# An attention layer's last pair of heads: output projection inside the slots, all blocks turned on VectorE, divisions in smaller groups

## The chip, the cores and the metric

The kernel runs on one core of one Trainium2 chip. The metric is the device time of one execution in microseconds (us); lower is better. All arithmetic is in 32-bit floating point.

## The reference

Two layers over 4096 nodes with 512 features each. Layer 0 is an additive graph attention, layer 1 is a masked dot-product attention with 8 heads of 64. Both add their result to their input.

```python
# layer 1, on h = relu(layernorm(x)), x of 4096 x 512, adj of 4096 x 4096
keys    = einsum('nj,hjk->hnk', h, Wks)        # 8 heads of 64
queries = einsum('nj,hjk->hnk', h, Wqs)
values  = einsum('nj,hjk->hnk', h, Wvs)
atts = einsum('hqk,hmk->hqm', queries, keys) / 8
atts = atts - 1e16 * (1 - maximum(adj, eye))
atts = softmax(atts, axis=-1)
out = x + einsum('hqm,hmk,hko->qo', atts, values, Wo)
```

The change lies in layer 1 only: in its last part, where heads 6 and 7 are worked on, and in the product with Wo that ends the kernel.

## The kernel before

**Stages.** Layer 0 runs first, in three pairs of heads and then a fourth pair whose stage also makes keys, queries and values of layer 1. Then comes layer 1, the subject here, from about 2490 us to the end. Its work goes over HC = 4 *pairs* of heads. Each pair has NG = 32 *groups* of 128 queries, each group has GS = 4 *slots* of 32 queries, so a pair has SETS = 128 slots and the layer `total` = 512. One loop over s (L1205 and above) hands out the work of a slot, written out by hand: instructions are issued to each engine in the order of the program. In this text, slots are counted within the last pair: slot 0 of it is s = 384, and the tail begins at slot 128.

**One slot's work.** The 128 partitions hold 4 quarters of the 4096 keys times 32 queries; the free axis holds QK_ = 1024 keys, for two heads.
- `scores` (L997): TensorE makes the products of queries and keys into four PSUM tiles `sc` of 128x512, one slot's worth; the pool has four buffers.
- `masked` (L1013): VectorE adds the penalty tile `a` (loaded by SP from pen_d, 512 KB a slot, five slots ahead, pool "a" with six buffers), writes to the ring `t` in SBUF and keeps the minima.
- `parted` (L1022) on GpSimd, `smallest` (L1034 on TensorE, L1039 on VectorE): every second slot, the minimum over the four quarters.
- `exps` (L1050): ScalarE takes the exponential, in place, three slots behind, and keeps the sums in `sums`.
- `squares` (L1057): four slots behind, VectorE turns squares of 32x32 in the first VC = 768 columns of both heads (128x1536 elements).
- `turned` (L1065) and `taken` (L1072): the other 256 columns are turned on TensorE in 128x128 blocks, for two slots at a time into a PSUM tile `tr` of two banks, and copied back by ScalarE.
- `weighted` (L1083): eight slots behind, TensorE multiplies with the values, 32 products a slot, into the PSUM tile `o` of a group. Values for the columns turned on TensorE are loaded in another order of rows.
- `finish` (L1092): ScalarE copies `o` out, SP writes it to att_d in DRAM.

**Divisions.** The softmax is divided by its sums late. `due` puts a generator into a list when enough groups are made; `some_divided` carries it on by one step in each slot. `inverted` sums over quarters, inverts, turns and writes to inv_d. `scaled` loads att_d and the inverses, multiplies (GpSimd, L1134; for the last groups VectorE) and writes att_d back. In the last pair there are divisions of 16, 8 and 8 groups.

**The tail.** After the last slot, `projected` multiplies, for each of NB = 32 blocks of 128 rows, the four pairs' columns of att_d with Wo (`wot`): four products of 128x512 into one `sc` tile (L1188), VectorE adds them to the rows of x (L1191), and SP stores. `load_chunk` loads two blocks of att_d and of x at a time. In the first eight tail slots the weighted products of the last groups stand between the blocks.

Of the kernel before, what the change touches and what calls it, by code (L numbers as in the profile page):

```python
# [15 lines left out]
P = 128  # L16
# [7 lines left out]
def kernel(  # L24
# [76 lines left out]
    with tc.tile_pool(name="a0k", bufs=1) as pk, tc.tile_pool(name="a0v", bufs=4) as pv, tc.tile_pool(  # L101
# [68 lines left out]
        def exps(G, h):  # L170
            if h == 0:
                G.sm = psb.tile([P, 2], F32, name="sm")
            nc.scalar.activation(  # L173
                G.t[h], G.t[h], AF.Exp, bias=G.nm[h][:, NCH : NCH + 1], scale=-1.0,
                accum_out=G.sm[:, h : h + 1],
            )
# [286 lines left out]
        def step(n):  # L463
            return groups[n // 2], n % 2
# [126 lines left out]
    with tc.tile_pool(name="b0c", bufs=1) as pc, tc.tile_pool(name="b0a", bufs=4) as pa, tc.tile_pool(  # L591
# [42 lines left out]
        def load_values(i):  # L634
            v = pv.tile([P, MB, PR], F32, name="bv")
            for a in range(NS):
                rows = bass.ds(a * QK_ + i * MB * SQ, MB * SQ)
                nc.sync.dma_start(
                    v[bass.ts(a, SQ)], d1_d[rows, bass.ts(C3, PR)].rearrange("(n i) d -> i n d", i=SQ)
                )  # L640
            values.append(v)
# [257 lines left out]

    HF = QK_ // 2
    VC = 768
    NV = VC // SQ
    NT = (QK_ - VC) // P
    SG = NG // 2
    with tc.tile_pool(name="a1t", bufs=1) as pt, tc.tile_pool(name="a1k", bufs=4) as pkk, tc.tile_pool(
        name="a1v", bufs=GS
    ) as pv, tc.tile_pool(name="a1a", bufs=6) as pa, tc.tile_pool(name="a1q", bufs=2) as pq, tc.tile_pool(
        name="a1x", bufs=2  # L910
    ) as px, tc.tile_pool(name="a1s", bufs=6) as psb, tc.tile_pool(name="a1z", bufs=2) as pz, tc.tile_pool(name="a1at", bufs=3) as pat, tc.tile_pool(
        name="a1sc", bufs=4, space=PSUM
    ) as psc, tc.tile_pool(name="a1tr", bufs=1, space=PSUM) as ptr, tc.tile_pool(
        name="a1m", bufs=1, space=PSUM
# [4 lines left out]
        class Group:  # L919


            def __init__(self, c, g):
                self.c, self.g = c, g
                self.ring = (c * NG + g) % (RING // GS) * GS
                self.nm = {}
                self.parts = {}

# [9 lines left out]
                )  # L937
                keys[c].append(k)

        def load_values(c, i):  # L940

            v = pv.tile([P, MB, PR], F32, name="v")
            cols = bass.ts(c, PR)
            if i * MB < NV:
                for a in range(NS):
                    rows = bass.ds(a * QK_ + i * MB * SQ, MB * SQ)
                    nc.sync.dma_start(
                        v[bass.ts(a, SQ)], v_d[rows, cols].rearrange("(n i) d -> i n d", i=SQ)
                    )
            else:  # L950
                for m in range(NT):
                    nc.sync.dma_start(
                        v[:, bass.ts(m, NS), :],
                        v_d[:, cols].rearrange("(a m p) d -> m p a d", a=NS, p=P)[VC // P + m],
                    )
            values[c].append(v)
# [96 lines left out]
                )  # L1053

        def squares(G, k):
            u = t[:, G.ring + k, :, :VC].rearrange("p h (n j) -> p h n j", j=SQ)
            nc.vector.transpose(u, u)  # L1057

        def turned(G, k):
# [14 lines left out]
        def weighted(G, i):  # L1074
            if i == 0:
                G.o = po.tile([P, 512], F32, name="o")
            v = values[G.c][i]
            for b in range(MB):
                mb = i * MB + b

                at = mb * SQ
                for h in range(2):
                    nc.tensor.matmul(  # L1083
                        G.o[bass.ts(h, D), :P],
                        lhsT=v[:, b, bass.ts(h, D)],
                        rhs=t[:, bass.ds(G.ring, GS), h, bass.ds(at, SQ)],
                        start=(mb == 0), stop=(mb == NB - 1),
                    )

        def finish(G):  # L1090
            oT = px.tile([P, P], F32, name="oT")
            nc.scalar.copy(oT, G.o[:, :P])  # L1092
            nc.sync.dma_start(att_d[G.c, :, bass.ts(G.g, P)], oT)

        def inverted(c, g, n):

# [20 lines left out]

        def scaled(c, g, n):

            last = c == HC - 1 and g + n == NG  # L1120
            zs = []
            for i in range(n // 4):
                cols = bass.ds((g + 4 * i) * P, 4 * P)
                z = pz.tile([P, 2, 4 * P], F32, tag="z", name="z")
                nc.sync.dma_start(z[:, 0], att_d[c, :, cols])
                for h in range(2):
                    nc.sync.dma_start(z[bass.ts(h, D), 1], inv_d[c, h, cols].partition_broadcast(D))
                yield
                zs.append((cols, z))
                if i % 2 == 0:  # L1130
                    continue
                yield
                for cols, z in zs:
                    (nc.vector if last else nc.gpsimd).tensor_mul(z[:, 0], z[:, 0], z[:, 1])  # L1134
                yield
                for cols, z in zs:
                    nc.sync.dma_start(att_d[c, :, cols], z[:, 0])
                zs = []

        def divided(c, g, n):  # L1140
            yield from inverted(c, g, n)
            yield from scaled(c, g, n)

        divisions = []

        def due(made):

            c, g = divmod(made, NG)
            if g == 0 and 0 < c < HC:
                divisions.append(divided(c - 1, SG, SG))  # L1150
            elif g == 0 and c == HC:
                divisions.append(divided(c - 1, NG - SG // 2, SG // 2))
            elif g == SG:
                divisions.append(divided(c, 0, SG))
            elif (c, g) == (HC - 1, NG - SG // 2):
                divisions.append(divided(c, SG, SG // 2))

        def some_divided():
            for d in divisions[:1]:
                if next(d, d) is d:  # L1160
                    divisions.pop(0)

        ZR = 2
        chunks = []

        def load_chunk():

            i = len(chunks)
            if i >= (NG - SG // 2) // ZR:
                for d in divisions:  # L1170
                    for _ in d:
                        pass
                divisions.clear()
            if i < NB // ZR:
                at = pat.tile([P, HC, ZR * P], F32, name="at")
                nc.sync.dma_start(at, att_d[:, :, bass.ts(i, ZR * P)].rearrange("c p n -> p c n"))
                xt = pa.tile([P, ZR, DM], F32, tag="a", name="xt")
                nc.sync.dma_start(xt, x1_d[bass.ts(i, ZR * P), :].rearrange("(r p) d -> p r d", p=P))
                chunks.append((at, xt))

        def projected(j):
            if j >= NB:
                return
            i, r = divmod(j, ZR)
            at, xt = chunks[i]
            o = psc.tile([P, HF], F32, tag="sc", name="oo")
            for c in range(HC):
                nc.tensor.matmul(  # L1188
                    o, lhsT=at[:, c, bass.ts(r, P)], rhs=wot[:, c, :], start=(c == 0), stop=(c == HC - 1)
                )  # L1190
            nc.vector.tensor_add(xt[:, r], xt[:, r], o)  # L1191
            if j >= NB - ZR:
                nc.sync.dma_start(out[bass.ts(j, P), :], xt[:, r])
            elif r == ZR - 1:
                nc.sync.dma_start(out[bass.ts(i, ZR * P), :].rearrange("(r p) d -> p r d", p=P), xt)
                load_chunk()

        groups = [Group(c, g) for c in range(HC) for g in range(NG)]
        total = len(groups) * GS
# [12 lines left out]
        with tc.manual_schedule():  # L1212
# [6 lines left out]
                    pens[n] = penalty(*step(n))  # L1219

            AHEAD = 5
            rb = 0
            load_keys(0)
            for n in range(AHEAD):
                prefetch(n)
# [5 lines left out]
            for s in range(total + PROD + 3):  # L1231
# [11 lines left out]
                turn = 0 <= s - TURN < total  # L1243
                if turn:
                    squares(*step(s - TURN))
                turn = turn and (s - TURN) % 2

                if s % 2 and 0 <= s - 3 < total:
                    G, k = step(s - 3)
# [3 lines left out]
                n = s - PROD  # L1253
                if 0 < n <= total and n % GS == 0:
                    finish(groups[n // GS - 1])
                if s > total:
                    projected(rb)
                    rb += 1
                if s < total:
                    scs = scores(*step(s))  # L1260
                    masked(*step(s), scs, pens.pop(s))
# [1 line left out]
                    taken(*step(s - TURN), tr)  # L1263
                if 0 <= s - EXPS < total:
                    exps(*step(s - EXPS))
                if s + 2 < total:
                    made_penalty(*step(s + 2), pens[s + 2])
                if s % 2 and s < total:
# [2 lines left out]
                if 0 <= n < total:  # L1271
                    W, w = step(n)
                    weighted(W, w)

                if n > 1 and n % GS == 1:
                    due(n // GS)
                some_divided()
                if s == (HC - 1) * SETS + SETS // 2:
                    wot = pkk.tile([P, HC, DM], F32, tag="k", name="wot")
                    nc.sync.dma_start(wot, wo.rearrange("h d o -> (h d) o").rearrange("(c p) o -> p c o", p=P))  # L1280
                if s > total - AHEAD and len(chunks) < 3:
                    load_chunk()
                prefetch(s + AHEAD)

            for j in range(rb, NB):
                projected(j)
                some_divided()


# [26 lines left out]
```

## Time and profile before

| | |
|---|---|
| median of 3 runs | 4843.03 us (4842.26 to 4843.56) |
| the profiled execution's own time | 4839.5 us |
| its span, first to last instruction | 4837.7 us |
| mean granted TensorE clock | 0.986 (1.00 in the stretches shown of layer 1) |
| TensorE (PE) busy | 4660.0 us, 96% |
| VectorE (DVE) busy | 4439.3 us, 92% |
| ScalarE (ACT) busy | 3834.3 us, 79% |
| GpSimd (POOL) busy | 442.8 us, 9% |

The span is the time between the first and last instruction that the profile records; the execution's own time is a little longer. A line such as "4405.44 1.97 PE L1083 ... x32" of the timeline says: 32 instructions of that kind on TensorE began at 4405.44 us and were over 1.97 us later. Matmuls are pipelined, so records overlap, and the pace is read from start to start. PEld is the loading of the stationary operand. What stands in square brackets is the engine's idle time before it, and what ended that. The chain of waits follows the end of the execution back to what released it.

### The profile page before, as it was taken

What the parts mean: (1) busy time and instruction counts of PE and PEld (TensorE: products, weight loads), DVE (VectorE), ACT (ScalarE), POOL (GpSimd) and SP (SyncE); (2) the same over time, 40 slices, a digit from 0 to 9 for tenths busy, and PEclk for the clock granted to TensorE, in tenths of its full rate; (3) what the DMA queues carried; (4) which work ended last, traced back from release to release, by engine and by line L of the source; (5) the groups of instructions that cost most, each with busy time, mean ns of one, the idle gap of its engine ahead of it and who ended that gap; (6) DMA issues with size and microseconds to landing.
All of it is one profiled execution on the core that took longest, in us unless ns stands there. A gap on an engine that the chain in (4) does not pass through costs nothing.

```text
span 4837.7 us, 145786 instructions
## 1 busy us (share of the span) xinstructions
PE 4660.0 (96%) x62102; PEld 3477.0 (72%) x62102; DVE 4439.3 (92%) x7788; ACT 3834.3 (79%) x4301; POOL 442.8 (9%) x1001
## 2 busy tenths in 40 slices
PE   8999999999999959999989999999999999999999
PEld 7888888888888847777756666666666666666664
DVE  7999999999999899888749999999999999999992
ACT  7999999999999898888748888666666666666660
POOL 2000000000000011101123343000000000000000
PEclk9999999999999979999999999999999999999999
DMA  7444544445444384444377787534444343533445
GB/s 267 155 164 150 183 169 162 158 150 202 159 161 150 118 182 145 143 143 144 111 218 252 252 273 263 190 131 148 140 159 160 132 157 130 193 132 130 163 133 197
DMA packets 358605, 818.49 MB, mean 169 GB/s; under 512 B 60096, under 2 KB 179136, under 8 KB 332864
## 3 DMA queue, kind: packets, MB, share of 16 engines
q1 hardware_dynamic: 357952, 809.16, 50.8%
q8 instruction: 486, 7.96, 0.7%
q14 instruction: 167, 1.37, 0.1%
HBM read 668.21 MB, written 140.77 MB: 167 GB/s over the span
## 4 chain that ended last, share of the span: by engine, by line
PE 60%; DVE 16%; ACT 14%; issue 8%; DMA 2%; SPq 1%; POOL 0%; DVEq 0%; ACTq 0%; POOLq 0%
PE o L1083 20%; PE sc L997 19%; ACT t L173 6%; DVE t L163 6%; PE tr L1065 5%; PE mp L793 5%; DVE pT L197 4%; ACT t L152 4%; ACT pT L195 2%; PE bo L716 2%; PE oo L1188 2%; DVE bt L669 2%; PE tr L186 2%; PE o L208 2%; DVE bt L708 2%
## 5 line engine op out<-in xcount | busy, mean ns | idle before, releaser
L1013 DVE CUSTOM_DVE_ANT_0 t<-sc,a 128x512 f32<-128x512 f32 x2048 | 1284.4, 682 | 88.7 <-PE sc L997 66.8
L1083 PEld LDWEIGHTS o<-t,v 128*64 128x64 f32 x16384 | 883.8, 137 | 429.2 <-issue 343.9
L1050 ACT ACTIVATE t<-t,nm 128x1024 f32<-128x1024 f32 x1024 | 1166.0, 1142 | 4.2 <-DVE nm L1039 3.5
L997 PE MATMUL sc<-k,q 64*32 64x512 f32 x16384 | 1004.6, 596 | 5.3 <-DVE nm L1013 5.1
L1083 PE MATMUL o<-t,v 128*64 128x128 f32 x16384 | 1007.4, 276 | 1.2 <-ACT oT L1092 1.2
L1057 DVE STREAM_TRANSPOSE t<-t 128x1536 f32<-128x1536 f32 x512 | 907.6, 1773 | 9.1 <-ACT t L1050 8.9
L163 DVE CUSTOM_DVE_ANT_0 t<-t,a 128x2048 f32<-128x2048 f32 x384 | 877.2, 2284 | 23.4 <-ACT t L152 19.1
L186 PE MATMUL tr<-ident,t 128*128 128x128 f32 x6144 | 779.4, 277 | 31.3 <-ACT pT L195 20.2
L208 PE MATMUL o<-pT,v 128*64 128x128 f32 x12288 | 756.8, 276 | 0.9 <-DVE pT L197 0.7
L186 PEld LDWEIGHTS tr<-ident,t 128*128 128x128 f32 x6144 | 662.5, 141 | 122.9 <-issue 65.4
L173 ACT ACTIVATE t<-t,nm 128x4096 f32<-128x4096 f32 x192 | 732.9, 3817 | 10.5 <-DVE nm L168 10.4
L152 ACT ACTIVATE t<-tb,src 128x4096 f32<-128x4096 f32 (+1 forms) x193 | 733.4, 3800 | 2.2 <-DVE tb L408 2.2
L1072 ACT COPY t<-tr 128x1024 f32<-128x1024 f32 x256 | 259.1, 1012 | 589.5 <-PE tr L1065 589.4
L208 PEld LDWEIGHTS o<-pT,v 128*64 128x64 f32 x12288 | 664.2, 137 | 61.7 <-issue 48.1
L197 DVE COPY pT<-tr 128x1024 f32<-128x1024 f32 x549 | 653.5, 1216 | 9.8 <-PE tr L186 9.8
L997 PEld LDWEIGHTS sc<-k,q 64*32 64x32 f32 x16384 | 251.6, 106 | 383.0 <-issue 330.9
L669 DVE CUSTOM_DVE_ANT_0 bt<-lk,ba 128x1024 f32<-128x1024 f32 x256 | 302.8, 1219 | 64.1 <-ACT e L799 45.2
L659 ACT ACTIVATE lk<-tb,srcb 128x1024 f32<-128x1024 f32 x256 | 283.8, 1116 | 74.5 <-DVE nm L669 65.7
L708 DVE STREAM_TRANSPOSE bt<-bt 128x2048 f32<-128x2048 f32 x128 | 295.1, 2306 | 0.0
L701 ACT ACTIVATE bt<-bt,nm 128x1024 f32<-128x1024 f32 x256 | 290.1, 1134 | 0.0
L1065 PE MATMUL tr<-ident,t 128*128 128x128 f32 x2048 | 280.4, 280 | 0.0
L716 PE MATMUL bo<-bt,bv 128*64 128x128 f32 x4096 | 257.7, 280 | 9.0 <-ACT boT L725 7.7
(124 smaller groups left out, 3656.7 us busy)
## 6 DMA issues: line engine op xcount, KB each, us to landing
a<-in_adj_dram SPq DMA_DIRECT2D x192, 1024.0 KB
a<-pen_d SPq DMA_DIRECT2D x384, 512.0 KB
ba<-in_adj_dram SPq DMA_DIRECT2D x512, 128.0 KB
a<-in_adj_dram SPq DMA_DIRECT2D x512, 128.0 KB
pen_d<-a SPq DMA_DIRECT2D x128, 512.0 KB
h<-hT_d SPq DMA_DIRECT2D x96, 256.0 KB
qk_d<-e SPq DMA_DIRECT2D x64, 256.0 KB
x<-in_x_dram SPq DMA_DIRECT2D x8, 1024.0 KB
```

The costliest lines, as they stand in the source:

```text
L152: nc.scalar.activation(tpart, targets[G.c, h][:, cols], AF.Prelu, bias=src[:, G.g, 2 * G.c + h : 2 * G.c + h + 1], alpha=SLOPE,)
L163: nc.vector.tensor_tensor_reduce(out=t, in0=t, in1=rows_of_adj[G, f], scale=-1.0, scalar=FMAX, op0=ALU.add, op1=ALU.min, accum_out=nm[:, f ...
L173: nc.scalar.activation(G.t[h], G.t[h], AF.Exp, bias=G.nm[h][:, NCH : NCH + 1], scale=-1.0, accum_out=G.sm[:, h : h + 1],)
L186: nc.tensor.transpose(tr[:, bass.ts(b % 4 * 2 + h, P)], G.t[h][:, bass.ts(i * MB + b, P)], ident)
L197: nc.vector.tensor_copy(pT, tr)
L208: nc.tensor.matmul(G.o[h * D : (h + 1) * D, :P], lhsT=feats[G.c][i][:, b, bass.ts(h, D)], rhs=pT[:, bass.ts(b % 4 * 2 + h, P)], start=(mb ...
L997: nc.tensor.matmul(sc[h][bass.ts(a, SQ), :], lhsT=G.q[bass.ts(h, D), bass.ds(G.q0 + k * SQ, SQ)], rhs=keys[G.c][half][bass.ts(h, D), a, :] ...
L1013: nc.vector.tensor_tensor_reduce(out=t[:, G.ring + k, h, cols], in0=scs[half][h], in1=a[:, cols], scale=1.0, scalar=FMAX, op0=ALU.add, op1 ...
L1050: nc.scalar.activation(u, u, AF.Exp, bias=G.nm[k // 2][:, k % 2, h : h + 1], scale=-1.0, accum_out=G.sm[:, h, k : k + 1],)
L1057: nc.vector.transpose(u, u)
L1065: nc.tensor.transpose(tr[:, j, h, bass.ts(m, P)], t[:, G.ring + k - 1 + j, h, bass.ds(VC + m * P, P)], ident,)
L1083: nc.tensor.matmul(G.o[bass.ts(h, D), :P], lhsT=v[:, b, bass.ts(h, D)], rhs=t[:, bass.ds(G.ring, GS), h, bass.ds(at, SQ)], start=(mb == 0) ...
```

## The change

It does four things, all in the last pair of layer 1.
1. Groups from SW = 12 on (slot 48; turned four slots later, from slot 52 on) are not `mixed`: VectorE turns all 1024 columns (128x2048 elements), TensorE turns nothing there, ScalarE copies nothing back. Their last quarter of the values is loaded once more, in straight order, into a buffer of the keys' pool.
2. From slot 52 on, one product of the projection is issued in each slot, between `turned` and `scores`, where the block's columns are loaded (`ready`, `load_chunk`). Blocks alternate between the two banks of the former `tr` tile. When a block is whole, ScalarE copies it to `oc` and GpSimd adds it to the rows of x, which come from the pool of the penalties; the store follows in the next slot. From slot 128 on whole blocks are issued as before, into `sc` tiles, added by VectorE.
3. The last pair is divided in 8, 8, 8, 4 and 4 groups.
4. The last four groups' columns of this pair aren't written to att_d: they are copied into an SBUF tile `final`, multiplied there on VectorE, and used as the product's operand directly.

```diff
+    SW, LAST = 12, 4
...
+                self.mixed = c < HC - 1 or g < SW
...
         def squares(G, k):
-            u = t[:, G.ring + k, :, :VC].rearrange("p h (n j) -> p h n j", j=SQ)
+            u = t[:, G.ring + k, :, : VC if G.mixed else QK_].rearrange("p h (n j) -> p h n j", j=SQ)
...
-            v = values[G.c][i]
+            v = values[G.c][i if G.mixed or i * MB < NV else GS]
...
         def finish(G):
+            if G.c == HC - 1 and G.g >= NG - LAST:
+                if not final:
+                    final.append(pz.tile([P, 2, 4 * P], F32, tag="z", name="z"))
+                nc.scalar.copy(final[0][:, 0, bass.ts(G.g - NG + LAST, P)], G.o[:, :P])
+                if G.g == NG - 1:
+                    nc.vector.tensor_mul(final[0][:, 0], final[0][:, 0], final[0][:, 1])
+                return
...
         def divided(c, g, n):
             yield from inverted(c, g, n)
             yield from scaled(c, g, n)
+            if c == HC - 1:
+                ready[0] = g + n
+
+        def last_divided():
+
+            c, g = HC - 1, NG - LAST
+            yield from inverted(c, g, LAST)
+            for h in range(2):
+                nc.sync.dma_start(
+                    final[0][bass.ts(h, D), 1],
+                    inv_d[c, h, bass.ds(g * P, LAST * P)].partition_broadcast(D),
+                )
+            yield
...
-            elif (c, g) == (HC - 1, NG - SG // 2):
-                divisions.append(divided(c, SG, SG // 2))
+            elif c == HC - 1 and g > 0 and g % 8 == 0:
+                divisions.append(divided(c, g - 8, 8))
+            elif c == HC - 1 and g == NG - LAST:
+                divisions.append(divided(c, g - 4, 4))
...
+        def load_chunk(ahead):
             i = len(chunks)
...
+            if i < NB // ZR and i <= ahead and (ready[0] >= ZR * (i + 1) or ZR * i >= NG - LAST):
+                C = HC if ZR * i < NG - LAST else HC - 1
                 at = pat.tile([P, HC, ZR * P], F32, name="at")
+                nc.sync.dma_start(at[:, :C], att_d[:C, :, bass.ts(i, ZR * P)].rearrange("c p n -> p c n"))
+                chunks.append(at)
+
+        def load_rows(j):
+            if j < NB and j not in xts:
+                xts[j] = pa.tile([P, QK_], F32, tag="a", name="xt")[:, :DM]
+                nc.sync.dma_start(xts[j], x1_d[bass.ts(j, P), :])
+
+        def projection():
+
+            for j in range(NB):
+                i, r = divmod(j, ZR)
+                here = not alone
+                if here:
+                    if not acc:
+                        acc.append(ptr.tile([P, 2, 2, NT * P], F32, name="tr"))
+                    o = acc[0][:, j % 2].rearrange("p h m -> p (h m)")
+                else:
+                    o = psc.tile([P, HF], F32, tag="sc", name="oo")
+                for c in range(HC):
+                    if c == 1:
+                        load_rows(j)
+                    if c == HC - 1 and j >= NG - LAST:
+                        at = final[0][:, 0, bass.ts(j - NG + LAST, P)]
+                    else:
+                        at = chunks[i][:, c, bass.ts(r, P)]
+                    nc.tensor.matmul(o, lhsT=at, rhs=wot[:, c, :], start=(c == 0), stop=(c == HC - 1))
+                    if c < HC - 1:
+                        yield None
+
+                def added(j=j, o=o):
+                    if here:
+                        oc = poc.tile([P, DM], F32, name="oc")
+                        nc.scalar.copy(oc, o)
+                        nc.gpsimd.tensor_add(xts[j], xts[j], oc)
+                    else:
+                        nc.vector.tensor_add(xts[j], xts[j], o)
+
+                yield added
+                nc.sync.dma_start(out[bass.ts(j, P), :], xts[j])
+
+        def whole_block():
+            for ahead in range(4):
+                load_rows(rb[0] + ahead)
+            load_chunk(rb[0] // ZR + 1)
+            load_chunk(rb[0] // ZR + 1)
+            added = None
+            while added is None:
+                added = next(products)
+            added()
+            rb[0] += 1
...
-                turn = turn and (s - TURN) % 2
+                turn = turn and (s - TURN) % 2 and step(s - TURN)[0].mixed
...
-                if s > total:
-                    projected(rb)
-                    rb += 1
+                added = None
+                if s >= total:
+                    if not alone:
+                        alone.append(1)
+                    if rb[0] < NB:
+                        whole_block()
+                elif s - TURN >= total - SETS + SW * GS and rb[0] // ZR < len(chunks):
+                    added = next(products)
+                    if added:
+                        rb[0] += 1
...
                     exps(*step(s - EXPS))
+                if added:
+                    added()
...
+                if s == total + EXPS:
+                    divisions.append(last_divided())
+                if s == total - SETS + 4 * GS:
                     wot = pkk.tile([P, HC, DM], F32, tag="k", name="wot")
...
+                    load_values(HC - 1, GS - 1, mixed=False)
+                if s > total - SETS:
+                    load_chunk(rb[0] // ZR + 1)
```

More of the change, by code (lines that the diff above doesn't have):

```diff
@@ L910 @@
         name="a1x", bufs=2
-    ) as px, tc.tile_pool(name="a1s", bufs=6) as psb, tc.tile_pool(name="a1z", bufs=2) as pz, tc.tile_pool(name="a1at", bufs=3) as pat, tc.tile_pool(
+    ) as px, tc.tile_pool(name="a1s", bufs=6) as psb, tc.tile_pool(name="a1z", bufs=2) as pz, tc.tile_pool(name="a1at", bufs=3) as pat, tc.tile_pool(name="a1oc", bufs=1) as poc, tc.tile_pool(
         name="a1sc", bufs=4, space=PSUM
@@ L938, in load_keys, with load_values @@
                 keys[c].append(k)
-        def load_values(c, i):
-            v = pv.tile([P, MB, PR], F32, name="v")
+        def load_values(c, i, mixed=True):
+            if mixed:
+                v = pv.tile([P, MB, PR], F32, name="v")
+            else:
+                v = pkk.tile([P, 2, MB, PR], F32, tag="k", name="vs")[:, 0]
             cols = bass.ts(c, PR)
-            if i * MB < NV:
+            if i * MB < NV or not mixed:
                 for a in range(NS):
@@ L1093, in finish @@
             nc.sync.dma_start(att_d[G.c, :, bass.ts(G.g, P)], oT)
+        final = []
         def inverted(c, g, n):
@@ L1118, in scaled @@
         def scaled(c, g, n):
-            last = c == HC - 1 and g + n == NG
             zs = []
@@ L1129, in scaled @@
                 zs.append((cols, z))
-                if i % 2 == 0:
+                if i % 2 == 0 and i < n // 4 - 1:
                     continue
@@ L1133, in scaled @@
                 for cols, z in zs:
-                    (nc.vector if last else nc.gpsimd).tensor_mul(z[:, 0], z[:, 0], z[:, 1])
+                    nc.gpsimd.tensor_mul(z[:, 0], z[:, 0], z[:, 1])
                 yield
@@ L1138, in scaled @@
                 zs = []
+        ready = [0]
         def divided(c, g, n):
@@ L1150, in due @@
                 divisions.append(divided(c - 1, SG, SG))
-            elif g == 0 and c == HC:
-                divisions.append(divided(c - 1, NG - SG // 2, SG // 2))
-            elif g == SG:
+            elif c < HC - 1 and g == SG:
                 divisions.append(divided(c, 0, SG))
-            elif (c, g) == (HC - 1, NG - SG // 2):
-                divisions.append(divided(c, SG, SG // 2))
+            elif c == HC - 1 and g > 0 and g % 8 == 0:
+                divisions.append(divided(c, g - 8, 8))
+            elif c == HC - 1 and g == NG - LAST:
+                divisions.append(divided(c, g - 4, 4))
         def some_divided():
@@ L1164 @@
         chunks = []
-        def load_chunk():
+        xts = {}
+        alone = []
+        acc = []
+        def load_chunk(ahead):
             i = len(chunks)
[L1169 to L1174, printed above, removed]
-                at = pat.tile([P, HC, ZR * P], F32, name="at")
[L1176 to L1196, printed above, removed]
+            if i < NB // ZR and i <= ahead and (ready[0] >= ZR * (i + 1) or ZR * i >= NG - LAST):
+                C = HC if ZR * i < NG - LAST else HC - 1
+                at = pat.tile([P, HC, ZR * P], F32, name="at")
+                nc.sync.dma_start(at[:, :C], att_d[:C, :, bass.ts(i, ZR * P)].rearrange("c p n -> p c n"))
+                chunks.append(at)
@@ new lines, in load_rows @@
+        def load_rows(j):
[27 more added lines that the diff above has]
+                        nc.gpsimd.tensor_add(xts[j], xts[j], oc)
+                    else:
+                        nc.vector.tensor_add(xts[j], xts[j], o)
+                yield added
+                nc.sync.dma_start(out[bass.ts(j, P), :], xts[j])
@@ L1198 @@
+        rb = [0]
+        products = projection()
+        def whole_block():
[8 more added lines that the diff above has]
+            rb[0] += 1
         groups = [Group(c, g) for c in range(HC) for g in range(NG)]
@@ L1221 @@
             AHEAD = 5
-            rb = 0
             load_keys(0)
@@ L1277 @@
                 some_divided()
-                if s == (HC - 1) * SETS + SETS // 2:
+                if s == total + EXPS:
+                    divisions.append(last_divided())
+                if s == total - SETS + 4 * GS:
                     wot = pkk.tile([P, HC, DM], F32, tag="k", name="wot")
                     nc.sync.dma_start(wot, wo.rearrange("h d o -> (h d) o").rearrange("(c p) o -> p c o", p=P))
-                if s > total - AHEAD and len(chunks) < 3:
-                    load_chunk()
+                    load_values(HC - 1, GS - 1, mixed=False)
+                if s > total - SETS:
+                    load_chunk(rb[0] // ZR + 1)
                 prefetch(s + AHEAD)
-            for j in range(rb, NB):
-                projected(j)
-                some_divided()
+            while rb[0] < NB:
+                whole_block()
+            next(products, None)
 _INS = [
```

## The prediction

> **What bounds the kernel now.** I read the page's engine line first (PE busy 96%, VectorE 92%, ScalarE 79%), then the busy times by stretch of time, for the shares mix stages:
>
> ```profile
> core 0: us, PE busy (x) PEld busy (x) DVE busy (x) ACT busy (x) POOL busy (x), PEclk, DMA share, GB/s
> 4500.00:4600.00 100.00, 100.00 (x1629) 63.18 (x1636) 97.13 (x220) 66.53 (x111) 5.38 (x14) 1.00 0.41 139
> 4707.00:4837.00 130.00, 126.55 (x497) 61.50 (x495) 28.58 (x40) 7.33 (x13) 0.00 (x0) 1.00 0.55 183
> ```
>
> The first row lies in the slots of the last pair: TensorE has no gap, VectorE works 97%, the granted clock is full. The second is the tail after the last slot: TensorE again, all others mostly idle. The end of the chain of waits says the same:
>
> ```profile
> 4754.16 3.49 PE oo L1188 x8
> 4757.82 75.74 PE oo L1188 x176
> ```
>
> 176 instructions of the output projection (two per product, eight per block of 128 rows) in one piece: 75.74/176 = 0.430 us each, 0.86 a product, 3.44 a block, with no wait. So I count TensorE's work, and ask whether VectorE still keeps up. The timeline gives two neighbouring slots. On TensorE:
>
> ```profile
> 4400.55 1.97 PE L1083 MATMUL o<-t,v 128*64 128x128 f32 x32
> 4402.35 0.26 PE L1034 MATMUL nmB<-parts,bands 128*64 128x32 f32 x4
> 4402.54 1.09 PE L1065 MATMUL tr<-ident,t 128*128 128x128 f32 x8
> 4403.56 1.95 PE L997 MATMUL sc<-k,q 64*32 64x512 f32 x32
> 4405.44 1.97 PE L1083 MATMUL o<-t,v 128*64 128x128 f32 x32
> 4407.34 1.95 PE L997 MATMUL sc<-k,q 64*32 64x512 f32 x32
> 4409.21 1.97 PE L1083 MATMUL o<-t,v 128*64 128x128 f32 x32
> ```
>
> From start to start (durations overlap): 1.80 + 0.19 + 1.02 + 1.88 + 1.90 + 1.87 = 8.66 us for a pair of slots. The eight transposes take 1.02 of it. VectorE over the same slots:
>
> ```profile
> 4402.64 1.77 DVE L1057 STREAM_TRANSPOSE t<-t 128x1536 f32<-128x1536 f32 x1
> 4404.34 0.15 DVE L1039 TENSOR_REDUCE nm<-nmB 128x4 f32<-128x32 f32 x1
> 4404.74 0.69 DVE L1013 CUSTOM_DVE_ANT_0 t<-sc,a 128x512 f32<-128x512 f32 x1 [0.25 <-PE sc L997]
> ...
> 4407.19 1.77 DVE L1057 STREAM_TRANSPOSE t<-t 128x1536 f32<-128x1536 f32 x1
> 4408.89 0.65 DVE L1013 CUSTOM_DVE_ANT_0 t<-sc,a 128x512 f32<-128x512 f32 x1
> ```
>
> Turn 1.70, reduce and wait 0.40, four masks 2.45, turn 1.70, four masks 2.41: also 8.66, of which only the 0.25 that waits for the scores is spare. Two rows of the groups price the turn of 1536 and of 2048 elements (the second in the stage before, with the same instruction):
>
> ```profile
> L1057 DVE STREAM_TRANSPOSE t<-t 128x1536 f32<-128x1536 f32 x512 | 907.6, 1773 | 9.1 <-ACT t L1050 8.9
> L708 DVE STREAM_TRANSPOSE bt<-bt 128x2048 f32<-128x2048 f32 x128 | 295.1, 2306 | 0.0
> ```
>
> **The slots from 52 on.** The pair has slots 0 to 127; from 52 to 127 there are 76, or 38 pairs of them. Out go the eight TensorE transposes of each: -1.02. In come two products. A product is 0.86 in a row of its own kind, but here it stands alone between other forms. A block between weighted products starts at 4707.32 (its first weight load) and the next work at 4710.96: 3.64, that is 3.44 and 0.20 for changing form. I take 0.86 + 0.19 = 1.05 for each, ends 0.86 and 1.10. The pair becomes 8.66 - 1.02 + 2.10 = 9.74, or 1.08 longer: 38 x 1.08 = **41.0 us more**. With 0.86 it would be 9.36, with 1.10 9.84 (45 us).
>
> VectorE's two turns grow by 2306 - 1773 = 0.533 each: 8.66 + 1.07 = 9.73 if the wait of 0.25 stays, 9.48 without it. So it fits into 9.74, with almost nothing over. ScalarE adds a bound of its own: the reduce at 4404.34 releases two exponentials, whose last record ends at 4407.01, and the turn that needs them starts at 4407.19. From reduce to that turn takes some 2.8, against 0.15 + 2.41 = 2.56 for VectorE alone; so even without the wait for scores VectorE's pair hardly gets below 9.7. That is the floor on the other side: the products can't come out much cheaper than I take them.
>
> The Trainium skill, "TensorE: Matmul & The Clock Gate", section on what happens when a matmul is issued, says that weight loads are pulled ahead of running matmuls, so that the change of form would be hidden. By that the product is 0.86 and VectorE's floor of 9.7 decides, which gives 40 instead of 41 us; the 0.20 above speaks for an open change here.
>
> **The tail.** 76 products are 19 blocks: 19 x 3.44 = 65.4 us leave it, and the two groups of transposes that stood there, 0.82 each by their starts: **67.0 us less**. Thirteen blocks stay, and the eight groups of weighted products between them. The last block's add and store come behind the last product as now.
>
> **Divisions.** Of 16, 8 and 8 groups become 8, 8, 8, 4 and 4. Within the slots that is four inversions in place of two: each takes some 0.5 us of TensorE (rows tot 0.33, invT 0.24) and a reciprocal of 0.51 on VectorE in place of one of 0.94. **+1.0 us**, ends 0 and 3.
>
> **What costs nothing, and by what cover.**
> - ScalarE loses 40 copies of 1.01 and gets 19 of 0.57 (row e<-mp, 128x512 out of PSUM). It is busy 66%; the copy is queued behind the exponentials of its slot. If it were on the way of VectorE: 19 x 0.57 = 11 us.
> - GpSimd gets 19 additions of 128x512. The nearest row, z<-z of the same shape, takes 1.29; at 4626.42 two of them run beside a turn and two masks that keep their 1.77 and 0.65 to 0.69, so VectorE isn't slowed. The addition waits for ScalarE's copy and for the row of x, and the small product "parts" is queued behind it, for which TensorE's nmB waits two slots later. Counted from the reduce: copy done about 3.4, addition 4.8, parts 5.1; nmB starts about 7.5. The cover is 2.4 us.
> - SP gets per block a load of x, a store, half a load of att, all in its one queue ahead of the penalties. The store waits for GpSimd's addition; behind it is a penalty load that is needed five slots (24 us) later. The x rows share the six buffers with the penalties, so a penalty waits for its predecessor's mask and has four slots (19 us), against 3.44 us that one such load held up the chain elsewhere (a<-in_adj_dram). Bytes: 14 MB more over some 370 us, 40 GB/s on 140; the tail moves 183 without holding TensorE up.
> - Blocks are ready at slots 47, 79 and 111, needed at 52, 84 and 116; output weights and the straight values are loaded at slot 16.
> - The last four groups: the sums inverted in tail slots 132 to 134, the scale loaded two slots before it is used; the copy (0.27) and the product (0.69) stand beside block 27 (3.44). If not covered, 2 to 5 us once.
>
> **The sum.** -67.0 + 41.0 + 1.0 = -25 us. The profiled execution took 4839.5 us (span 4837.7), 3.5 below the median of 4843.0; the difference is carried to the median: **4818**. The gain is not the overlap: a product in a slot costs 1.05 and saves 0.86 in the tail. It is the transposes that leave a full TensorE.
>
> The Trainium skill, "VectorE: DVE Perf Modes", section Rules for kernel authors, gives 128x128 transposes to TensorE where PSUM will do. Here both ways cost the same by rows (1.02 against 1.07 a pair of slots), on engines that are both nearly full.
>
> **Rivals.**
> 1. *VectorE and TensorE wait in turn.* If each slot keeps a wait of 0.25 for its scores, VectorE's pair is 9.98: 38 x 1.32 = 50, so -16: **4827**. For it: four PSUM buffers of scores are one slot's worth, and both engines stand within 0.3 us of each other. Against it: scores are begun 1.2 us ahead of the first mask, and now TensorE never waits for a buffer.
> 2. *Slower: GpSimd's queue.* The addition comes late (row of x or copy), "parts" behind it, and TensorE waits at nmB. The stage before has just this: "PE nmB L685 <- POOL parts L676: 37.0, 7, 8.5", over 16 blocks of two groups, 2.3 us each. 19 x 2.3 = 44: +19, **4862**. It decides from 1.3 us per block over the cover of 2.4, so from an addition that ends 3.7 us later than counted. Against it: there GpSimd had a chain of six instructions, here one; x is asked for two slots ahead.
> 3. *Faster:* the change of form is hidden and the wait with ScalarE vanishes: 9.48 a pair, 31 us: -35, **4808**.
> 4. *It doesn't do what it says:* an att load lands late and TensorE stands at a product. Five slots of lead speak against it; three such stalls of 5 us give -10, 4833.
>
> **How the numbers follow.** Forecast (4811 to 4825) 0.50; rival 1 0.18; rival 3 0.12; rival 4 0.05; rival 2 0.15. A measurement of this kernel tells 0.2% (9.7 us) from no change. Faster by more: 0.50 + 0.12, most of rival 1 and a part of 4, 0.75; within 0.10; slower 0.15. The range runs from TensorE's own cheapest pair, 9.36 (27 - 67 + 1 = -39, 4804), to a slot 0.87 longer, where nothing is gained (4843); rival 2 and a little more lie outside.
>
> **What would show it.** Right: in the slots, a pair about 9.74 us, TensorE still 100%, VectorE over 97%; in the tail no idle TensorE, and about 66 us from the last slot's end to the end of the span. Wrong: a pair over 10.4 (all gain gone), nmB waiting for parts, masks waiting for scores by more than 0.25, TensorE idle ahead of block 28 or a product waiting for att.

## The result, and the profile after

The changed kernel takes 4825.85 us (median; 4822.78 to 4827.19) against 4842.56 of the kernel before in the same measurement: ratio 0.9965, 95% interval 0.9953 to 0.9978. That is 16.7 us or 0.35% faster, where 25 us were forecast.

The stages tell more than the whole. VectorE turns once in every slot, so the starts of its turns mark the slots, and each stretch can be read from the timeline (us; "four slots" is the mean over slots 88 to 99, where no division stands except in the last kernel). The kernels below the second line are those of the experiments, with the number of the experiment.

| kernel | slots 0-51 | slots 52-127 | tail | slot 0 to end | four slots |
|---|---|---|---|---|---|
| before | 226.3 | 331.4 | 133.8 | 691.5 | 17.32 |
| changed | 227.5 | 378.8 | 66.0 | 672.3 | 19.84 |
| 1: e1_copy_first | 227.5 | 373.4 | 66.1 | 667.0 | 19.50 |
| 3: e2_turn_only | 227.5 | 361.1 | 129.4 | 717.9 | 18.95 |
| 5: e3_two_a_pair | 227.5 | 366.3 | 66.1 | 659.8 | 19.10 |
| 4: e4_overlap_only | 227.5 | 403.2 | 67.7 | 698.3 | 21.07 |
| 2: e5_two_tiles | 227.5 | 373.4 | 66.0 | 666.9 | 19.50 |
| 6: e6_from_slot_32 | 237.5 | 368.5 | 48.2 | 654.1 | 19.47 |

From slot 0 to the end the change is worth 691.5 - 672.3 = 19.2 us: +1.1, +47.4 and -67.7. Ahead of slot 0 these kernels do the same work (experiments 2 and 4 split one copy in two), but the first pair of layer 1 took anything from 544.8 to 552.4 us in the eight profiles (546.7 before, 550.3 changed). So single profiles are best compared from slot 0 on.

Busy time by stretch, the slots and the tail:

```profile
4500.00:4600.00 100.00, 98.62 (x1370) 52.60 (x1376) 96.86 (x191) 50.86 (x94) 11.85 (x19) 1.00 0.51 169
4758.00:4824.00 66.00, 62.65 (x379) 33.74 (x375) 19.49 (x23) 8.59 (x19) 1.48 (x2) 1.00 0.39 132
```

The tail has halved. In the slots TensorE has fallen from 100.00 to 98.62: something makes it wait that did not before. The timeline of TensorE over two pairs of slots shows what:

```profile
4603.63 1.13 PE L1230 MATMUL tr<-wot,at 128*128 128x512 f32 x2
4604.69 1.95 PE L1003 MATMUL sc<-k,q 64*32 64x512 f32 x32
4606.57 1.97 PE L1089 MATMUL o<-t,v 128*64 128x128 f32 x32
4608.46 1.13 PE L1230 MATMUL tr<-wot,at 128*128 128x512 f32 x2
...
4613.38 1.12 PE L1230 MATMUL tr<-wot,at 128*128 128x512 f32 x2
...
4618.56 1.12 PE L1230 MATMUL tr<-wot,at 128*128 128x512 f32 x2 [0.28 <-ACT oc L1237]
```

A product starts 1.06 us ahead of the scores behind it (4603.63 to 4604.69), as priced, and a pair of slots takes 4613.38 - 4603.63 = 9.75 us. But once in four slots, at the first product of a block, TensorE stands until ScalarE has copied the block before. The list of waits from 4430 to 4750 us (slots 62 to 126) has it 16 and 13 times; the figures are us in total, times and the longest, the first line for gaps of the weight loads, the second for those of the multiplications:

```profile
PEld tr L1230 <- ACT oc L1237: 7.4, 16, 0.5
PE tr L1230 <- ACT oc L1237: 3.6, 13, 0.3
```

Over all of slots 52 to 127 it is 18 and 15 times, 8.5 and 4.1 us.

On ScalarE the copy stands behind the two exponentials of its slot, and these behind a long wait for VectorE's minimum. The last line is TensorE's next product:

```profile
4436.33 1.15 ACT L1056 ACTIVATE t<-t,nm 128x1024 f32<-128x1024 f32 x1 [5.11 <-DVE nm L1045]
...
4437.47 1.13 ACT L1056 ACTIVATE t<-t,nm 128x1024 f32<-128x1024 f32 x1
...
4438.61 0.56 ACT L1237 COPY oc<-tr 128x512 f32<-128x512 f32 x1
...
4439.22 1.12 PE L1230 MATMUL tr<-wot,at 128*128 128x512 f32 x2 [0.27 <-ACT oc L1237]
```

The copy is over at 4439.17, and the product starts at 4439.22. ScalarE had stood idle for 5.11 us just before the two exponentials.

### The profile page after: what moved, and what is told of

Its sections match the earlier page's. It is cut to its first block, busy times and chain, and to the rows that moved or that the text cites. A ratio compares the mean times of both kernels' runs of the same rounds, so it can differ in the third digit from the quotient of the medians.

```text
span 4824.4 us, 145215 instructions
## 1 busy us (share of the span) xinstructions
PE 4640.8 (96%) x61788; PEld 3441.7 (71%) x61788; DVE 4472.5 (93%) x7773; ACT 3805.7 (79%) x4282; POOL 467.8 (10%) x1021
## 4 chain that ended last, share of the span: by engine, by line
PE 57%; DVE 16%; ACT 14%; issue 9%; DMA 3%; SPq 1%; POOL 0%; DVEq 0%; ACTq 0%; POOLq 0%
PE o L1089 19%; PE sc L1003 19%; ACT t L173 6%; DVE t L163 6%; PE mp L793 5%; DVE pT L197 4%; PE tr L1071 4%; ACT t L152 4%; ACT pT L195 2%; PE bo L716 2%; DVE bt L669 2%; PE tr L186 2%; PE o L208 2%; DVE bt L708 2%; PE tr L1230 1%
## 5 line engine op out<-in xcount | busy, mean ns | idle before, releaser
L1089 PEld LDWEIGHTS o<-t,v 128*64 128x64 f32 x15744 | 850.8, 137 | 414.8 <-issue 328.0
L1089 PE MATMUL o<-t,v 128*64 128x128 f32 x15744 | 969.6, 276 | 2.9 <-ACT oT L1105 2.9
L1063 DVE STREAM_TRANSPOSE t<-t 128x1536 f32<-128x1536 f32 (+1 forms) x512 | 950.1, 1856 | 10.0 <-ACT t L1056 9.8
L186 PE MATMUL tr<-ident,t 128*128 128x128 f32 x6144 | 779.1, 277 | 30.3 <-ACT pT L195 20.2
L1078 ACT COPY t<-tr 128x1024 f32<-128x1024 f32 x216 | 218.9, 1013 | 481.3 <-PE tr L1071 481.1
L195 ACT COPY pT<-tr 128x1024 f32<-128x1024 f32 x219 | 241.3, 1102 | 14.1 <-PE tr L186 13.9
```

Of the source, the lines that this page charges most:

```text
L186: nc.tensor.transpose(tr[:, bass.ts(b % 4 * 2 + h, P)], G.t[h][:, bass.ts(i * MB + b, P)], ident)
L1089: nc.tensor.matmul(G.o[bass.ts(h, D), :P], lhsT=v[:, b, bass.ts(h, D)], rhs=t[:, bass.ds(G.ring, GS), h, bass.ds(at, SQ)], start=(mb == 0) ...
```

## Experiments

**1. The copy ahead of the exponentials.**

```diff
+                if added:
+                    added()
                 if 0 <= s - EXPS < total:
                     exps(*step(s - EXPS))
-                if added:
-                    added()
```

> ScalarE's copy of a finished block stands ahead of the slot's exponentials and not behind them; nothing else differs from the changed kernel. Theory (the first product of the next block waits for that copy, 0.35 us on TensorE per block): the four-slot period falls from 19.84 to 19.49 us, slots 52 to 127 take 372.5 us for 378.8, the whole about 4819.5. Rival (VectorE is the bound and the wait only takes up time that the masks would wait anyway): the period stays at 19.8, the whole stays at 4826.

Measured: 4821.28 us, ratio to the kernel before 0.9952 (0.9939 to 0.9964). Four slots take 19.50, slots 52 to 127 373.4, 5.4 us less than in the changed kernel. TensorE's row reads 100.00 again:

```profile
4500.00:4600.00 100.00, 100.00 (x1412) 54.08 (x1398) 98.19 (x198) 51.72 (x92) 11.32 (x17) 1.00 0.53 173
```

From slot 0 to the end this kernel takes 24.5 us less than before: the 25 that the sum had for the change without this wait.

**2. Two tiles in place of one.** The blocks alternate between the two banks of one PSUM tile, so the next block doesn't overwrite what ScalarE is copying. Here the copy stays late, but the banks are two tiles.

```diff
-                        acc.append(ptr.tile([P, 2, 2, NT * P], F32, name="tr"))
-                    o = acc[0][:, j % 2].rearrange("p h m -> p (h m)")
+                        acc.append(ptr.tile([P, 2, NT * P], F32, name="tr"))
+                        acc.append(pac.tile([P, 2, NT * P], F32, name="ac"))
+                    o = acc[j % 2].rearrange("p h m -> p (h m)")
```

> The changed kernel with its late copy, but the two PSUM banks in which the blocks alternate are two tiles and not the halves of one (up to slot 52 the transposes fill the same two tiles, and ScalarE copies each by itself). Theory (the next block waits for the copy only because both halves are one tile to whatever places the waits): the wait goes, four slots take 19.50 us for 19.84, slots 52 to 127 about 373 us, the whole about 4820. Rival (TensorE waits for ScalarE for another reason, the end of the copy being needed anyway): four slots stay at 19.84, the whole at 4826.

Measured: 4820.14 us, ratio 0.9949 (0.9936 to 0.9963); four slots 19.50, slots 52 to 127 373.4, and no wait of TensorE for ScalarE's copy is left in the list, although the copy stands as late as before. So the wait was not one for data. It was there because both banks belonged to one tile, and either edit removes it. The Trainium skill, "PSUM — Partial Sum Buffer", summary of rules, says to let a matmul run into another bank than the one being read; here another bank was not enough, it had to be another tile.

**3. VectorE's turns alone.** All 32 blocks stay in the tail.

```diff
-                elif s - TURN >= total - SETS + SW * GS and rb[0] // ZR < len(chunks):
+                elif False:
```

> VectorE turns all columns from slot 52 on as in the changed kernel, but no product goes into the slots: all 32 blocks stand in the tail. Theory (gain from TensorE's total, with VectorE nearly full): VectorE alone sets the pace of the slots, 9.5 to 9.73 us a pair of slots for 8.66, so 31 to 41 us more there, the tail 1.6 us shorter than before: 4871 to 4882, slower than before. Rival (taking the transposes from TensorE is a gain by itself): 7.64 us a pair, 39 us less: about 4803.

Measured: 4869.34 us, ratio 1.0054 (1.0041 to 1.0068), slower than before and just under the range expected. A pair of slots takes 18.95 / 2 = 9.47 us, although TensorE has only 7.64 us of work in it. So VectorE's floor is 9.47, just under the 9.5 to 9.73 expected. Its row reads 100.00 (the line is in the last section), and TensorE waits for buffers of scores instead, here in the list of waits from 4400 to 4700 us:

```profile
PEld sc L1003 <- DVE nm L1019: 86.7, 214, 0.5
```

**4. The overlap alone.** Products go into the slots, while TensorE goes on turning its 256 columns, slot by slot. One bank holds the four transposes, the other the block.

```diff
-                self.mixed = c < HC - 1 or g < SW
+                self.mixed = True
...
-                turn = turn and (s - TURN) % 2 and step(s - TURN)[0].mixed
+                single = s - TURN >= total - SETS + SW * GS
+                turn = turn and (single or (s - TURN) % 2)
...
-                    tr = turned(*step(s - TURN))
+                    tr = turned(*step(s - TURN), (0,) if single else (0, 1))
```

> One product in each slot from slot 52 on, but TensorE goes on turning the last 256 columns, four transposes in every slot there (one PSUM bank holds them, the other holds the product; before slot 52 the two banks are copied by two copies of half the size). Copy-first as well. Theory (the overlap by itself is no gain: a product costs more in a slot than in the tail): 8.66 - 1.02 + 2 x (0.41 + 0.86 + 0.20) = 10.58 us a pair of slots, 73 us more in the slots, 65 less in the tail: about 4851, slower than before. Rival (the overlap is the gain, products fill gaps between the other work): at most 9.75 us a pair, 4818 or less.

Measured: 4849.3 us, ratio 1.0013 (1.0004 to 1.0022): a little slower than before. A pair of slots takes 10.53 us, and from slot 0 to the end it is 698.3 for 691.5. Neither half of the change is a gain alone. The transposes off TensorE leave room that VectorE's floor hides (experiment 3), and the products without that room cost more in the slots than they save in the tail. TensorE's timeline also shows what the 0.2 us belongs to:

```profile
4597.07 0.66 PE L1072 MATMUL tr<-ident,t 128*128 128x128 f32 x4
4597.57 1.02 PE L1233 MATMUL ac<-wot,at 128*128 128x512 f32 x2
4598.52 1.95 PE L1003 MATMUL sc<-k,q 64*32 64x512 f32 x32
```

The four transposes and the product have the same form of weights, 128*128, and from their start to the scores it is 1.45 us: 0.41 + 0.86, and 0.18 once. So it is a cost of a stretch of one form, not of each kind of instruction in it.

**5. Two products in every second slot**, with the copy first.

```diff
-                elif s - TURN >= total - SETS + SW * GS and rb[0] // ZR < len(chunks):
-                    added = next(products)
+                elif s - TURN >= total - SETS + SW * GS and rb[0] // ZR < len(chunks) and s % 2:
+                    for _ in range(2):
+                        added = next(products)
```

> As the copy-first kernel, but two products in every second slot instead of one in each. Theory (each stretch of products costs a change of form of 0.19 us on TensorE): 9.55 us a pair of slots by TensorE, held up by VectorE's floor somewhere between 9.5 and 9.73, so 1 to 7 us less than copy-first: 4813 to 4818. Rival (the change of form is no cost of its own, or VectorE's floor is 9.73): the same as copy-first, about 4819.

Measured: 4815.68 us, ratio 0.994 (0.9928 to 0.9952). Four slots take 19.10, 0.20 a pair less than copy-first: one change of form fewer in each pair. On TensorE's timeline the two products stand as one stretch from 4597.31 to the scores at 4599.23, 1.92 = 2 x 0.86 + 0.20:

```profile
4597.12 0.26 PE L1040 MATMUL nmB<-parts,bands 128*64 128x32 f32 x4
4597.31 1.98 PE L1230 MATMUL tr<-wot,at 128*128 128x512 f32 x4
4599.23 1.95 PE L1003 MATMUL sc<-k,q 64*32 64x512 f32 x32
```

**6. From slot 32 on.** If a block costs less in the slots than in the tail, more blocks belong there. Divisions by four groups make them ready earlier; in the tail four blocks are spread over the slots ahead of the last division.

```diff
-    SW, LAST = 12, 4
+    SW, LAST = 7, 4
...
-            elif c == HC - 1 and g > 0 and g % 8 == 0:
-                divisions.append(divided(c, g - 8, 8))
-            elif c == HC - 1 and g == NG - LAST:
+            elif c == HC - 1 and g > 0 and g % 4 == 0:
                 divisions.append(divided(c, g - 4, 4))
...
-                    if rb[0] < NB:
+                    if rb[0] < NB and (s - total in (0, 2, 5, 8) or s > total + PROD):
                         whole_block()
```

> As two-a-pair, but VectorE's turns and the products begin at slot 32, with divisions by four groups throughout, so that 24 blocks and not 19 stand in the slots; in the tail the four blocks ahead of the last division are spread over its slots. Theory (a block costs 1.78 us in the slots at a pace of 19.10 per four slots for 17.32, and 3.44 in the tail; a division 0.75): five blocks give 8.3, three more divisions take 2.2: 6 us less than two-a-pair, 653.7 us from slot 0 of the pair to the end for 659.8, the whole about 4810. Rival (columns come too late when asked for two or three slots ahead, or the last division is no longer covered): TensorE stands before a product, and the stretch is 660 us or more.

Measured: 4806.27 us, ratio 0.9924 (0.9911 to 0.9938), and 654.1 us from slot 0 to the end for the 653.7 worked out. It is the fastest of all, 38 us under the kernel before on the same chip (4844.26). That the sum came out so closely is in part luck. Four slots with a division take 20.20 for 19.10, so a division costs 1.1 and not 0.75, and the slots grew by 12.2 us for the 11.1 of the theory; the tail shrank by 17.9 for 17.2.

## Why the prediction was right or wrong, by its steps

The mechanism held: the gain comes from transposes that leave a full TensorE, and experiments 3 and 4 show that neither half gains alone. One wait was missing from it. So the measured 4826 lies just above the 4811 to 4825 of the forecast, within the wide range of 4804 to 4843, and two thirds of the 25 us came. With the copy first, which takes that wait away, the terms from slot 0 on are +41.4 for the pairs of slots (19 x 2.18), +1.7 for the divisions and -67.7 for the tail, beside +41.0, +1.0 and -67.0 in the sum. Two of the signs of being wrong did show: TensorE read 98.62 and not 100, and masks waited 0.51 us for scores.

**The pair of slots: right.** 9.74 us were worked out for it, and 9.75 stand in the timeline for a pair without the wait; with it the mean is 9.92, and with the copy first 19.50 / 2 = 9.75. The term that was least sure, 0.19 for the change of form, is confirmed by experiment 5 (0.20 less when one is taken away); what in the change takes that time is not shown. The Trainium skill, "TensorE: Matmul & The Clock Gate", section on what happens when a matmul is issued, lets a weight load be pulled ahead only where the row groups do not conflict or a background buffer takes it; the prediction left these conditions out. For these forms the 0.20 us was not hidden.

**The tail: right.** -67.0 us worked out, -67.7 measured, and the last four groups kept on the chip hold nothing up:

```profile
4803.22 6.28 PE L1230 MATMUL oo<-wot,at 128*128 128x512 f32 x14
4809.33 1.02 PE L1230 MATMUL oo<-wot,z 128*128 128x512 f32 x2
4810.19 2.74 PE L1230 MATMUL oo<-wot,at 128*128 128x512 f32 x6
```

The first product from `final` (z) follows block 27 and its own three others without an idle time.

**The divisions: within their range, but each costs twice what was counted.** In the kernel before, four slots with a division of eight groups take 18.45 us for 17.32: 1.13, where 0.5 was counted from TensorE's rows alone. There are four in place of two, one more in slots 0 to 51 (+1.1) and three in place of two behind them. That makes +1.7 with the copy first, for +1.0 forecast. In the changed kernel four slots with a division take 20.59 for 19.84, so 0.75 each, presumably because part of it falls into the wait for the copy.

**ScalarE's copy: the step that failed.** It stood among what costs nothing, with 11 us if it were on VectorE's way. It was on TensorE's way, and cost 5.4. I asked who needs the copied data (GpSimd), not who needs the copied buffer, and took the other bank for free. The exponentials that it is queued behind were named, but not the wait of 5 us that these stand in. The masks' waits for scores grew as an echo (0.51 us at 4601.05): in slots 52 to 127 they are 10.7 us in all, and 6.0 with the copy first. That the measured 4826 lies beside rival 1's 4827 is chance. In rival 1 VectorE and TensorE wait for each other in every slot; what the runs show is one slot in four that loses 0.34 us through ScalarE, and none with the copy first or with two tiles. One argument against rival 1 was read too strongly, though: "TensorE never waits for a buffer" holds for its multiplications in the slots, but in the kernel before weight loads of scores waited for VectorE 36 times there, 6.2 us in all.

**VectorE's floor: wrong, without effect on the sum.** 9.7 was put there because some 2.8 us lay between the reduce (4404.34) and the turn that needs its exponentials (4407.19). But that turn follows the last mask without an idle time: 0.25 of the stretch is VectorE's wait for scores and the other 2.60 its own work. The exponentials were over 2.67 us after the reduce, and a part of this was ScalarE's copy of the transposes, behind which they stood:

```profile
4403.72 1.01 ACT L1072 COPY t<-tr 128x1024 f32<-128x1024 f32 x1 [3.11 <-PE tr L1065]
4404.63 1.15 ACT L1050 ACTIVATE t<-t,nm 128x1024 f32<-128x1024 f32 x1
```

The change removes this copy. After it, the exponentials are over 2.56 us after the reduce (4605.73), and the turn starts at 4608.32, 2.59 us after it. A chain that runs through a removed instruction must be counted anew, and of two things that end ahead of a start the later one sets it: before the change this was the last mask, not the exponentials. With the floor at 9.47 a cheaper pair was possible: experiment 5 came to 9.55, near rival 3's 9.48, but by one change of form fewer and not, as rival 3 has it, by a hidden one.

**GpSimd's queue: right.** In the same count from the reduce (4436.14), the addition ended at 4.4 (4.8 forecast) and parts at 4.6 (5.1), while nmB came at 7.8 (7.5). TensorE never waited for parts, so rival 2 did not occur. Nor did rival 4: no product waited for its columns.

**The remaining difference.** The profiles differ by 13.3 us, the medians by 16.7, the stretch from slot 0 on by 19.2. In these two profiles the changed kernel reaches slot 0 5.9 us later, 3.6 of it in the first pair, which varies by more than this among kernels with the same work there; what makes it vary was not studied.

## What to carry to other kernels

When two engines are both nearly full, price each half of a change for each engine: here moving work from TensorE to VectorE was slower alone, giving TensorE other work in the slots was slower alone, and both together were faster. For every new copy out of PSUM, ask who wants the buffer next as well as who wants the data, and issue it where its engine stands idle, ahead of instructions that will wait. Count the changes between forms of matmul as work: putting two alike side by side saved 0.20 us each time.

## What the runs showed that was not expected

A TensorE row of 100% is no proof that it sets the pace. With VectorE's turns alone, both engines read 100.00 in the slots, though TensorE's work was 7.64 of 9.47 us: the records of multiplications that wait for a buffer between them are drawn out (32 products of scores in 2.92 us for 1.95), and only the waits of the weight loads show it. The busy times by stretch, first TensorE, third VectorE:

```profile
4500.00:4600.00 100.00, 100.00 (x1400) 51.97 (x1402) 100.00 (x202) 49.51 (x90) 5.12 (x13) 1.00 0.39 123
```

On its timeline, the scores of one slot:

```profile
4593.09 2.92 PE L1003 MATMUL sc<-k,q 64*32 64x512 f32 x32
```

The Trainium skill, "Perfetto Trace Analysis", section on identifying the most-contended engine, calls matmul busy time a poor measure and advises the busy share of weight loads; here that fell from 63.18 (before) to 51.97, with fewer loads in a longer pair of slots, while the busy time said nothing. But it does not decide the question either: with the copy first, where taking work from TensorE still shortened the slots (experiment 5), it reads 54.08.
